# One PSUM bank for X, Y and N; four score tiles; score matmuls of two heads in turns

## The chip, the cores and the metric

The kernel runs on one core of a Trainium2 chip. A core has five engines with queues of their own: TensorE (PE in the profile; its weight loads are listed as PEld), VectorE (DVE), ScalarE (ACT), GpSimd (POOL) and SyncE (SP), which here only issues DMAs. TensorE writes its results to PSUM, an on-chip memory that this kernel fills with eight tiles, each a bank of up to 512 fp32 columns over 128 partitions. In this kernel DVE and ACT read and write PSUM; POOL and the DMAs work on the other on-chip memory, SBUF. The metric is the device time of one execution in microseconds (us).

## What is computed

Input x is 4 sequences of 512 positions with 512 channels; cond is one 512-vector per sequence. Three layers, each added to its input, stand one behind the other:

```python
# 1. attention, 16 heads of 32: q and k are RMS-normed per head
qkv  = (rms_norm(x, g_norm) * (1 + scale) + shift) @ W_qkv   # scale, shift = split(cond @ W_emb + b_emb)
o    = softmax(q @ k.T * 32**-0.5) @ v
x1   = x + o + o @ W_out
# 2. GRU over the 512 positions, one after the other; state starts at cond
gi, gh = x1[:, t] @ W_ih + b_ih, h @ W_hh + b_hh
r, z = sigmoid(i_r + h_r), sigmoid(i_z + h_z)
n    = tanh(i_n + r * h_n)
h    = (1 - z) * n + z * h
x2   = x1 + hs
# 3. two causal convolutions over time, 4 taps taken from cond, each added; the second has a bias
x3   = x2 + conv(x2, cond);  out = x3 + conv(x3, cond) + b
```

The GRU is sequential: position t + 1 needs the state of position t. Attention of a block of positions needs K and V of all positions, but Q of its own block alone.

## The kernel before

**Stages.** A first stage normalises x, builds K and V for all positions and splits the weights into fp16 pairs. Then the attention of block 0 is run (a block is 32 positions of all 4 sequences, so 128 rows; there are 16 blocks). Then come the 512 steps of the GRU (the loop at L1180, 'the scan'). Attention, output projection and input gates of blocks 1 to 15 and the convolutions of finished blocks are put between the steps.

**One step of the scan.** The program emits, in this order:
1. Fillers for DVE, ACT and POOL (`q_.head`, L1196).
2. 32 matmuls into `X` (gates r and z, L1203 to L1206), then 32 into `Y` (gate n, L1209 to L1212). They add onto a seed that ACT wrote into the same columns in the step before. Four matmuls with 32 output partitions each go side by side.
3. DVE transposes `X` into `TX` (L1214) and adds two halves into `S` (L1216). ACT takes the tanh, `ZT` (L1217), writes the next seed into `X` (`seedX`, L1219, with the instruction at L1099), and makes `d0` (L1220).
4. DVE transposes `Y` into `TY` (L1226) and combines it with ZT in a scan whose result `NN` lies in PSUM (L1227). ACT takes the tanh of NN (`D1`, L1228) and writes the next seed into `Y` (`seedY`, L1231, with the instruction at L1102).
5. TensorE's fillers (`q_.pe`, L1235) and, where they have few columns, a matmul of zeros that keeps TensorE busy (`keep_warm`, L1236, with the instruction at L241).
6. DVE makes the new state: `A` (L1237) and `HS` (L1238). The next step's matmuls into `X` need A.

**PSUM.** `X`, `NN` and `Yb` (with `Y` in its first 128 columns and `idle`, a place for matmuls of zeros, in the rest) are three tiles, and each tile takes a bank. Two banks are tiles with tag `m` (transposes, projections), two with tag `s` (scores), one with tag `O` (attention output).

**What orders the accesses.** The program has no semaphores written by hand. The framework records for each tile which engine reads or writes it, in program order, and makes the waits.

**Planner.** `Queue` (L58) holds tasks sorted by priority. A task acquires tiles by tag, has chunks for TensorE, each with a cost in the planner's own units, and then stages on DVE, ACT or POOL with a budget per step (L37). In a step, `pe` (L128) issues chunks in order of priority as long as their costs fit into `SLOT0` = 1300 units for the first 64 steps and `PE_SLOT` = 1150 after them. The tasks of a block's attention: Q and R (queries and their norms), for each of 16 heads S (scores: three chunks of four matmuls with 32 x 512 results, one per sequence; then a row maximum `mx` on DVE at L442 and an exponential on ACT at L451), TP (transposes, then a copy on ACT at L471) and AV (the product with V), at the end ON, TO, WO and GI (output projection, gates). A block that isn't done in time is flushed: its rest is issued at once (L190). The attention of block 0 runs through the same planner before the scan, with 1300 units per round (L1060).

**The end of block 0.** `tail` (L597) projects block 0 in four column groups j: `wo(j)` writes columns j of the PSUM tile `pw` (L520, L521, L631), `x1(j)` reads columns j three times: ACT at L634, DVE at L635, ACT at L636.

Of the kernel before, what the change touches and what calls it, by code (L numbers as in the profile page):

```python
# [8 lines left out]
F32 = mybir.dt.float32  # L9
# [7 lines left out]
P = 128  # L17
# [2 lines left out]
WS = 256.0  # L20
IWS = 1.0 / WS
KS_SCALE = 32.0
PE_SLOT = 1150
SC_ = 100
SLOT0, NS0 = 1300, 64
OFF2 = 120
WARM = 384
GI_T = 2
# [4 lines left out]
          TX=(245, 0), LK=(159, 1.1), S=(4, 4.8), TP=(52, 4.7), AV=(115, 2.6))  # L33
PR1 = dict(PR, ON=(305, 0), TO=(-313, 0), WO=(-28, 0), GI=(-131, 0),
           LK=(128, 0.3), S=(67, 5.1), TP=(100, 6.1), AV=(-432, 6.6))
COLS = {SC_: 192, 230: 256, 138: 192, 137: 64, 109: 128, 330: 128, 111: 256, 108: 256}
DVE_B, ACT_B, POOL_B = 1130, 1900, 3300  # L37


# [123 lines left out]
def body(ctx, tc, x, cond, W_emb, b_emb, g_norm, W_qkv, g_q, g_k, W_out, W_ih, W_hh, b_ih, b_hh, L3_b, out):  # L163
    nc = tc.nc
# [4 lines left out]
    pg = ctx.enter_context(tc.tile_pool(name="pg", bufs=1, space=PS))  # L169
    pb = ctx.enter_context(tc.tile_pool(name="pb", bufs=1, space=PS))  # L170

    X = pg.tile([P, 256], F32, name="X")
    NN = pg.tile([P, 16, 4], F32, name="N")
    Yb = pg.tile([P, 512], F32, name="Y")
    Y, idle = Yb[:, 0:128], Yb[:, 128:512]

    def pm(name):
        return pb.tile([P, 512], F32, name=name, tag="m", bufs=2)
# [59 lines left out]
    def keep_warm(n, to=None):  # L238

        for _ in range(n):  # L240
            nc.tensor.matmul(idle if to is None else to, zz[:, 0:128], zz[:, 0:384], start=to is not None, stop=True, skip_group_check=True)  # L241

    nc.tensor.matmul(Yb, zz[:, 0:128], zz, start=True, stop=True, skip_group_check=True)
    clear()

    XD = [drm.tile([P, 2, 4, B, P], F16, name=f"XD{k}") for k in range(4)]
# [65 lines left out]

    X1, XN_, XT_ = {}, {}, {}
    last = dict(S=[], TP=[], R=[])
    q_ = Queue(dict(m=2, s=2, O=1, P=4, PT=4, xb=3, xhl=1, QS=3, q=1, o=1, gi=1, x1=3, L=3))

    def block_tasks(i):
        first, pre_q = i == 0, i < 2
        tl = []
        s = {}  # L320
# [23 lines left out]
        def turn(dst, src, tag="m"):  # L344

            def piece(j):
                def f():
                    if j == 0:
                        s[dst] = pb.tile([P, 512], F32, name="pt_", tag=tag, bufs=2)
                    transpose4(s[dst], s[src], (j,))  # L350
                return f
            return [(109, piece(j)) for j in range(4)]

        MMS = [(a, w, k) for a, w in ((0, 0), (1, 0), (0, 1)) for k in range(4)]

# [22 lines left out]
            nc.vector.scalar_tensor_tensor(s["ql"], f4, IWS, s["qh"], ALU.mult, ALU.subtract)  # L378

        if not pre_q:  # L380
            Q = add(f"Q{i}", deps=[XT_[i // 4]] + last["R"], acq=["m", "q", "QS"], chunks=[(111, qch(j, u)) for j in range(4) for u in range(6)],
                    stages=[[("ACT", 960, qs0)], [("DVE", 600, qs1)]], rel=["m"] + (["xhl"] if i % 4 == 3 else []))

        def rch():
# [40 lines left out]
        prev_av = None  # L425

        def sch(j, q, u):
            def f():
                if u == 0:
                    s[("s", j, q)] = pb.tile([P, 512], F32, name="ps", tag="s", bufs=2)  # L430
                t = s[("s", j, q)]
                R_ = slice(32 * q, 32 * q + 32)
                x_, k_ = (("qh", KH), ("qh", KL), ("ql", KH))[u]
                for b in range(B):
                    nc.tensor.matmul(t[32 * b:32 * b + 32, :], s[x_][R_, j, 32 * b:32 * b + 32], k_[R_, j, b, :],  # L435
                                     start=(u == 0), stop=(u == 2), skip_group_check=True)
            return f

        def smax(j, q):
# [15 lines left out]
        def tpch(h, ps=False):  # L455
            def piece(j):
                def f():
                    if j == 0:
                        s[("pt", h)] = pb.tile([P, 512], F32, name="ptp", tag="s" if ps else "m", bufs=2)
                    transpose4(s[("pt", h)], s["PX"][h], (j,))  # L460
                return f
            return [(109, piece(j)) for j in range(4)]

        def tps(h):
            def f():
# [18 lines left out]
        for j in range(4):  # L484
            for q in range(4):
                h = 4 * j + q
                STask[h] = add(f"S{i}.{h}", h, deps=[R], acq=["s", "P"], after=last["S"], chunks=[(SC_, sch(j, q, u)) for u in range(3)],
                               stages=[[("DVE", 600, smax(j, q)), ("Pool", 150, lambda: None)], [("ACT", 720, sexp(j, q))]],
                               rel=["s"], settle=int(first))
                last["S"] = [STask[h]]  # L490
                TPs[h] = add(f"TP{i}.{h}", h, deps=[STask[h]], after=last["TP"], acq=["m", "PT"], chunks=tpch(h),
                             stages=[[("ACT", 490, tps(h))]], rel=["m", "P"], settle=int(first))
                last["TP"] = [TPs[h]]
                dep = [TPs[h]] + ([prev_av] if prev_av else [])
                AVs[h] = add(f"AV{i}.{h}", h, deps=dep, chunks=[(137, avch(h, kt)) for kt in range(4)],
                             acq=["O"] if h == 0 else [], rel=["PT"])
                prev_av = AVs[h]
# [49 lines left out]
        def chain():  # L547
            ON = add(f"ON{i}", deps=[AVs[15]], acq=["o"], stages=[[("DVE", 800, on)]], stage_lag=[1], rel=["O", "QS", "L"])

            TO = add(f"TO{i}", deps=[ON], acq=["m"], chunks=turn("pto", "o"), stages=[[("ACT", 480, tos), ("DVE", 600, lambda: None)]], rel=["m"], settle=1)  # L550
            WO = add(f"WO{i}", deps=[TO, LX], acq=["m", "x1"], chunks=[(230 if u < 0 else 111, woch(j, u)) for j in range(4) for u in range(-1, 6)],
                     stages=[[("ACT", 960, wos)], [("DVE", 600, wos1)]], rel=["m", "xb", "o"], settle=1)

            gis = []
            for g, n in enumerate("rzn"):
                def gch(g, n, part):
                    def f():
                        if part == 0:
                            s["pgi" + n] = pm("pgi")
                        c = slice(256 * (part // 12), 256 * (part // 12) + 256)  # L560
                        a, wi, k = MMS[part % 12]
                        nc.tensor.matmul(s["pgi" + n][:, c], s[("x1h", "x1l")[a]][:, k, :], WR[n][:, wi, k, c],
                                         start=(part % 12 == 0), stop=(part % 12 == 11))
                    return f

                def gst(g, n):
                    def f():
                        gs = at("gs", [P, 4, P])
                        pj = "p (j q s) -> p q j s"
                        nc.vector.tensor_tensor(gs.rearrange("p q (j s) -> p q j s", j=4), s["pgi" + n].rearrange(pj, j=4, q=4),  # L570
                                                bias[:, g].rearrange(pj, j=4, q=4), ALU.add)
                        nc.sync.dma_start(GD[i][:, :, :, g, :].rearrange("q b t c -> (b t) q c"), gs)
                    return f

                gis.append(add(f"GI{i}{n}", deps=[WO], acq=["m", "gi"], chunks=[(108, gch(g, n, p)) for p in range(24)],
                               stages=[[("DVE", 600, gst(g, n))]], rel=["m", "gi"], settle=1))

        if first:
# [18 lines left out]
        def tail(nx, ahead):  # L597
# [42 lines left out]
            def gik(k):  # L640
                for n in "rzn":
                    if k == 0:
                        pg[n] = pm("pgn") if n == "n" else pb.tile([P, 512], F32, name="pgi" + n, tag="s", bufs=2)
                    for m, (xa, wi) in enumerate(((xh, 0), (xl, 0), (xh, 1))):
                        nc.tensor.matmul(pg[n], xa[:, k, :], WR[n][:, wi, k, :], start=(k == 0 and m == 0), stop=(k == 3 and m == 2))

# [42 lines left out]
    with ExitStack() as pre_ctx:  # L689
# [81 lines left out]
            nc.scalar.activation(YS[i], XS[i], AF.Copy, scale=RS[:, i:i + 1])  # L771

        def x_t(i, tag=None):
            PY[i] = pb.tile([P, 512], F32, name="py", tag=tag, bufs=2 if tag == "s" else 1) if tag else pm("py")
            transpose4(PY[i], YS[i])

        def x_n(i, e):
# [121 lines left out]
        KV4 = {}  # L899

        def proj(v, kt, b):
            p = pb.tile([P, 512], F32, name="pkv", tag="s", bufs=2)
            XH, XL = XHL[kt]
            n = 0
            for k in range(4):
                for (xa, wi) in ((XH, 0), (XL, 0), (XH, 1)):
                    nc.tensor.matmul(p, xa[:, k, b, :], WKV[:, wi, k, v, :], start=(n == 0), stop=(n == 11))
                    n += 1
            return p
# [143 lines left out]
    x2b = [lt(f"x2b{i}", [P, 16, 35]) for i in range(2)]  # L1053
    x3b = [lt(f"x3b{i}", [P, 16, 35]) for i in range(2)]
    with tc.manual_schedule(engines={ENG.PE, ENG.DVE, ENG.Activation, ENG.Pool, ENG.SP}):
        ahead = [t for t in need[1] if t.name in ("S1.0", "S1.1", "S1.2")]
        late = [t for t in need[1] if t.name == "S1.3"]
        need[1] = [t for t in need[1] if t not in ahead + late]
        q_.add(need[0] + ahead)
        q_.flush(need[0] + ahead, 1300, lambda used: keep_warm(max(0, int((800 - used) / 160))), {8: scan_constants})  # L1060
        gs0 = bts[0]["tail"](bts[1], late)
    for i in range(1, NB):
        if i > 1:
# [51 lines left out]
    def conv_tasks(i):  # L1115
# [47 lines left out]
            nc.scalar.activation(ob, s["px4"], AF.Copy)  # L1163
            nc.sync.dma_start(out[:, 32 * i:32 * i + 32, :], ob)

        TX = Task(f"TX{i}", prio=100 * i + PR["TX"][0], deps=[C1], acq=["m"], chunks=[(109, toc(j)) for j in range(4)], stages=[[("ACT", 480, tos)]], rel=["m", "cv"])
        return [C1, TX]

    q_.free["cv"] = 1
# [101 lines left out]
```

## Time and profile before

| | |
|---|---|
| median of three executions | 1899.21 us (1896.22 to 1905.69) |
| profiled execution | 1898.34 us, of it a span of 1896.6 us from the first to the last instruction |
| busy, share of the span | PE 86%, DVE 77%, ACT 62%, PEld 61%, POOL 17% |
| A (L1237), one per step | first starts at 230.9 us, last at 1877.2 us: 3.22 us per step |
| the 32 X and 32 Y matmuls of a step (L1200) | X 273 ns each, Y 220 ns each; they overlap |
| TX, TY, N (DVE) | 447, 400, 301 ns |
| seed of X, of Y (ACT) | 396, 277 ns |
| one score matmul (L435) | 377 to 388 ns; four overlap |

How to read it: the span falls into about 231 us ahead of the first state, 511 distances from one state to the next, and some 19 us after the last. An idle time that is listed with an arrow names the instruction whose end released the engine. Times of the timeline are us from the start of the span.

### The profile page before, as it was taken

The numbers are of one execution on the slowest core, as the hardware profiler recorded it, in microseconds if no ns is written. First come the engines' busy times: TensorE is split into PE (matmuls) and PEld (weight loads), VectorE is DVE, ScalarE is ACT, GpSimd is POOL, SyncE is SP. The second block draws the span as 40 slices with busy tenths as digits, with TensorE's granted clock in tenths as the row PEclk, the third lists the DMA queues.
The fourth block names the chain that finished last, engine by engine and source line by source line (L and its number), as shares of the span: only waits on it lengthen the run. The fifth ranks groups of instructions, "written<-read, shape, count | busy, mean of one in ns | idle before, by whom it ended". The sixth has DMA issues, their size and how long they took to land. (4 is left out here: it accounts for less than half of the span.)

```text
span 1896.6 us, 113881 instructions
## 1 busy us (share of the span) xinstructions
PE 1633.8 (86%) x48944; PEld 1162.2 (61%) x48944; DVE 1453.0 (77%) x5315; ACT 1176.5 (62%) x4578; POOL 329.0 (17%) x1151
## 2 busy tenths in 40 slices
PE   5789899988899999999898989999898989987553
PEld 2444567666666666666666666666666666666442
DVE  4786477877888787878787887878787878887675
ACT  4544475766677666767575766666575757664442
POOL 1361011202111212111111111111111111111111
PEclk9999999999999999999999999999999999999998
DMA  5652011010100101010101011010101000001000
GB/s 187 221 186 112 24 51 35 22 43 19 29 24 16 34 19 54 13 39 11 38 14 31 20 35 38 21 31 11 40 13 39 12 26 19 23 24 27 16 17 9
DMA packets 68919, 78.09 MB, mean 41 GB/s; under 512 B 6560, under 2 KB 54720, under 8 KB 67776
## 3 DMA queue, kind: packets, MB, share of 16 engines
q1 hardware_dynamic: 68416, 70.82, 12.1%
q8 instruction: 384, 6.29, 1.4%
q14 instruction: 119, 0.97, 0.2%
HBM read 44.58 MB, written 26.21 MB: 37 GB/s over the span
## 5 line engine op out<-in xcount | busy, mean ns | idle before, releaser
L1200 PEld LDWEIGHTS <-BT 128*8 128x8 f16 (+1 forms) x24576 | 449.7, 89 | 69.4 <-issue 4.4
L1200 PE MATMUL X<-Wlo,A 128*4 128x256 f16 x8192 | 313.2, 273 | 187.8 <-DVE A L1237 145.4
L1217 ACT ACTIVATE ZT<-S 128x32 f32<-128x32 f32 x512 | 134.6, 263 | 503.0 <-DVE S L1216 503.0
L1214 DVE STREAM_TRANSPOSE TX<-X 128x256 f32<-128x256 f32 x512 | 228.7, 447 | 146.6 <-PE X L1200 146.3
L1242 POOL TENSOR_SCALAR hsb<-HS 128x16 f32<-128x16 f32 x512 | 115.0, 225 | 1241.5 <-DVE HS L1238 1221.4
L1200 PEld LDWEIGHTS <-A 128*4 128x4 f16 x8192 | 151.2, 83 | 282.7 <-DVE A L1237 260.1
L1200 PE MATMUL X<-Whi,BT 128*8 128x256 f16 x8192 | 315.3, 274 | 0.2 <-issue 0.2
L1200 PE MATMUL Y<-Whi,BT 128*16 128x128 f16 x8192 | 206.3, 220 | 1.5 <-issue 1.4
L1226 DVE STREAM_TRANSPOSE TY<-Y 128x128 f32<-128x128 f32 x512 | 204.8, 400 | 3.3 <-PE Y L1200 2.1
L1200 PE MATMUL Y<-Wlo,BT 128*16 128x128 f16 x8192 | 205.3, 220 | 0.8 <-issue 0.8
L1099 ACT ACTIVATE X<-G 128x256 f32<-128x256 f32 x510 | 202.1, 396 | 2.9 <-DMA G<-GD 1.4
L451 ACT ACTIVATE PX<-ps,nb,rqs 128x512 f32<-128x512 f32 x256 | 195.4, 763 | 10.8 <-DVE nb L443 5.8
L1227 DVE TENSOR_TENSOR_SCAN N<-ZT,TY 128x64 f32<-128x64 f32 x512 | 154.1, 301 | 54.8 <-ACT D L1220 1.8
L1237 DVE TENSOR_TENSOR_SCAN A<-D,D 128x32 f16<-128x32 f32 x512 | 115.3, 225 | 94.7 <-ACT D L1228 94.2
L442 DVE TENSOR_REDUCE mx<-ps 128x1 f32<-128x512 f32 x256 | 175.0, 684 | 11.4 <-PE ps L435 11.1
L297 PE MATMUL ptp<-ident,PX 128*128 128x128 f32 x1024 | 170.0, 288 | 1.3 <-DVE gs L570 0.6
L1109 ACT ACTIVATE BT<-A 128x64 f16<-128x64 f16 x512 | 131.0, 256 | 52.8 <-DVE A L1237 2.0
L297 PEld LDWEIGHTS ptp<-ident,PX 128*128 128x128 f32 x1024 | 110.4, 142 | 78.0 <-issue 61.6
L471 ACT ACTIVATE PT<-ptp 128x512 f32<-128x512 f32 x248 | 143.3, 584 | 12.8 <-PE ptp L297 12.7
L1102 ACT ACTIVATE Y<-G 128x128 f32<-128x128 f32 x510 | 141.2, 277 | 0.5 <-issue 0.3
L479 PEld LDWEIGHTS po<-V,PT 128*32 128x32 f32 x8192 | 95.3, 111 | 57.9 <-issue 53.4
L1216 DVE TENSOR_TENSOR S<-TX 128x32 f32<-128x32 f32 x512 | 114.8, 224 | 17.5
(257 smaller groups left out, 2754.9 us busy)
## 6 DMA issues: line engine op xcount, KB each, us to landing
GD<-gs SPq DMA_DIRECT2D x45, 256.0 KB
G<-GD SPq DMA_DIRECT2D x512, 16.0 KB
G<-GD SPq DMA_DIRECT2D x512, 8.0 KB
xp<-in_x_dram SPq DMA_DIRECT2D x16, 256.0 KB
xb<-in_x_dram SPq DMA_DIRECT2D x16, 256.0 KB
xhl<-XD SPq DMA_DIRECT2D x32, 128.0 KB
out_dram<-ob SPq DMA_DIRECT2D x16, 256.0 KB
wst<-in_L_cond_W_qkv_dram SPq DMA_DIRECT2D x6, 512.0 KB
```

Source lines behind the costliest of these rows:

```text
L297: nc.tensor.transpose(dst[:, 128 * j:128 * j + 128], src[:, 128 * j:128 * j + 128], ident)
L442: nc.vector.tensor_reduce(s["mx"][:, h:h + 1], s[("s", j, q)], AX.X, ALU.max)
L451: nc.scalar.activation(pe_, s[("s", j, q)], AF.Exp, bias=s["nb"][:, h:h + 1], scale=s["rqs"][:, h:h + 1], accum_out=s["ls"][:, h:h + 1])
L471: nc.scalar.activation(pt_, s[("pt", h)], AF.Copy)
L1099: nc.scalar.activation(X.rearrange("p (g c) -> p g c", g=2), G[(t // 4) % 2][:, t % 4, 0:2, :], AF.Copy)
L1102: nc.scalar.activation(Y, G[(t // 4) % 2][:, t % 4, 2, :], AF.Copy)
L1109: nc.scalar.activation(Bt[:, :, 1:8:2, :], A[:, :, 1].rearrange("p (k b) -> p k b", k=4).unsqueeze(2).to_broadcast([P, 4, 4, 4]), AF.Copy)
L1200: nc.tensor.matmul(dst[32 * qq:32 * qq + M, :], lhs, W[:, k, cols].rearrange("p g (j q s) -> p q g j s", j=4, q=4)[:, qq], start=False, st ...
L1214: nc.vector.transpose(TX.rearrange("p a r -> p (a r)"), X)
L1217: nc.scalar.activation(zt[:, :, :, 2], S.rearrange("p (g a) -> p g a", g=2), AF.Tanh, scale=0.5 * IWS)
L1226: nc.vector.transpose(TY.rearrange("p h j b k -> p j h k b"), Y.rearrange("p (j h k b) -> p j h k b", j=4, h=2, k=4))
L1227: nc.vector.tensor_tensor_scan(f(NN), f(zt[:, 0]), TY[:, 0].rearrange("p j b k -> p (j b k)"), 0.0, ALU.mult, ALU.add)
```

## The change

`X`, `Y`, `NN` and `idle` become column ranges of one tile, `XY`, of one bank. The two banks that come free go to the tag `s`, which now has four tiles. The scores of two heads are one task for TensorE: its three chunks take eight matmuls each, the two heads' matmuls in turns; each head's maximum and exponential stay tasks of their own, which depend on the pair. The pair acquires two `s` and two `P` at once. The costs of most chunks and the budgets of a step get other numbers: 1450 units for a step (1570 in the first 64), 225 for a pair's chunk of scores in place of twice 100, 150 for a transpose in place of 109, 140 for a chunk of Q in place of 111, 680 for the first chunk of each quarter of WO in place of 230, 123 for a chunk of GI in place of 108. A matmul of zeros into `idle` has 64 columns, not 384. The order of the instructions in a step is not changed, nor are the priorities.

```diff
-PE_SLOT = 1150
-SC_ = 100
-SLOT0, NS0 = 1300, 64
+PE_SLOT = 1450
+SC_ = 225
+SLOT0, NS0 = 1570, 64
...
-COLS = {SC_: 192, 230: 256, 138: 192, 137: 64, 109: 128, 330: 128, 111: 256, 108: 256}
+COLS = {SC_: 384, 680: 256, 137: 64, 150: 128, 330: 128, 140: 256, 111: 256, 123: 256}
...
-    X = pg.tile([P, 256], F32, name="X")
-    NN = pg.tile([P, 16, 4], F32, name="N")
-    Yb = pg.tile([P, 512], F32, name="Y")
-    Y, idle = Yb[:, 0:128], Yb[:, 128:512]
+    XY = pg.tile([P, 512], F32, name="XY")
+    X, Y = XY[:, 0:256], XY[:, 256:384]
+    NN = XY[:, 384:448].rearrange("p (a k) -> p a k", k=4)
+    idle = XY[:, 448:512]
...
-            nc.tensor.matmul(idle if to is None else to, zz[:, 0:128], zz[:, 0:384], start=to is not None, stop=True, skip_group_check=True)
+            o = idle if to is None else to
+            nc.tensor.matmul(o, zz[:, 0:128], zz[:, 0:o.shape[-1]], start=to is not None, stop=True, skip_group_check=True)
...
-    q_ = Queue(dict(m=2, s=2, O=1, P=4, PT=4, xb=3, xhl=1, QS=3, q=1, o=1, gi=1, x1=3, L=3))
+    q_ = Queue(dict(m=2, s=4, O=1, P=4, PT=4, xb=3, xhl=1, QS=3, q=1, o=1, gi=1, x1=3, L=3))
...
                 if u == 0:
-                    s[("s", j, q)] = pb.tile([P, 512], F32, name="ps", tag="s", bufs=2)
-                t = s[("s", j, q)]
-                R_ = slice(32 * q, 32 * q + 32)
+                    for r in (q, q + 1):
+                        s[("s", j, r)] = pb.tile([P, 512], F32, name="ps", tag="s", bufs=4)
                 x_, k_ = (("qh", KH), ("qh", KL), ("ql", KH))[u]
                 for b in range(B):
-                    nc.tensor.matmul(t[32 * b:32 * b + 32, :], s[x_][R_, j, 32 * b:32 * b + 32], k_[R_, j, b, :],
-                                     start=(u == 0), stop=(u == 2), skip_group_check=True)
+                    for r in (q, q + 1):
+                        R_ = slice(32 * r, 32 * r + 32)
+                        nc.tensor.matmul(s[("s", j, r)][32 * b:32 * b + 32, :], s[x_][R_, j, 32 * b:32 * b + 32], k_[R_, j, b, :],
+                                         start=(u == 0), stop=(u == 2), skip_group_check=True)
...
-                STask[h] = add(f"S{i}.{h}", h, deps=[R], acq=["s", "P"], after=last["S"], chunks=[(SC_, sch(j, q, u)) for u in range(3)],
+                if q % 2 == 0:
+                    SP = add(f"SP{i}.{h}", h, deps=[R], acq=["s", "s", "P", "P"], after=last["S"], chunks=[(SC_, sch(j, q, u)) for u in range(3)], settle=1)
+                    last["S"] = [SP]
+                STask[h] = add(f"S{i}.{h}", h, deps=[SP],
                                stages=[[("DVE", 600, smax(j, q)), ("Pool", 150, lambda: None)], [("ACT", 720, sexp(j, q))]],
                                rel=["s"], settle=int(first))
-                last["S"] = [STask[h]]
...
-        ahead = [t for t in need[1] if t.name in ("S1.0", "S1.1", "S1.2")]
+        ahead = [t for t in need[1] if t.name in ("SP1.0", "S1.0", "S1.1", "SP1.2", "S1.2")]
...
-        q_.flush(need[0] + ahead, 1300, lambda used: keep_warm(max(0, int((800 - used) / 160))), {8: scan_constants})
+        q_.flush(need[0] + ahead, 1700, lambda used: keep_warm(max(0, int((1050 - used) / 160))), {8: scan_constants})
```

More of the change, by code (lines that the diff above doesn't have):

```diff
@@ L240, in keep_warm @@
         for _ in range(n):
-            nc.tensor.matmul(idle if to is None else to, zz[:, 0:128], zz[:, 0:384], start=to is not None, stop=True, skip_group_check=True)
-    nc.tensor.matmul(Yb, zz[:, 0:128], zz, start=True, stop=True, skip_group_check=True)
+            o = idle if to is None else to
+            nc.tensor.matmul(o, zz[:, 0:128], zz[:, 0:o.shape[-1]], start=to is not None, stop=True, skip_group_check=True)
+    nc.tensor.matmul(XY, zz[:, 0:128], zz, start=True, stop=True, skip_group_check=True)
     clear()
@@ L351, in piece @@
                 return f
-            return [(109, piece(j)) for j in range(4)]
+            return [(150, piece(j)) for j in range(4)]
         MMS = [(a, w, k) for a, w in ((0, 0), (1, 0), (0, 1)) for k in range(4)]
@@ L380, in block_tasks @@
         if not pre_q:
-            Q = add(f"Q{i}", deps=[XT_[i // 4]] + last["R"], acq=["m", "q", "QS"], chunks=[(111, qch(j, u)) for j in range(4) for u in range(6)],
+            Q = add(f"Q{i}", deps=[XT_[i // 4]] + last["R"], acq=["m", "q", "QS"], chunks=[(140, qch(j, u)) for j in range(4) for u in range(6)],
                     stages=[[("ACT", 960, qs0)], [("DVE", 600, qs1)]], rel=["m"] + (["xhl"] if i % 4 == 3 else []))
@@ L458, in f @@
                     if j == 0:
-                        s[("pt", h)] = pb.tile([P, 512], F32, name="ptp", tag="s" if ps else "m", bufs=2)
+                        s[("pt", h)] = pb.tile([P, 512], F32, name="ptp", tag="s" if ps else "m", bufs=4 if ps else 2)
                     transpose4(s[("pt", h)], s["PX"][h], (j,))
                 return f
-            return [(109, piece(j)) for j in range(4)]
+            return [(150, piece(j)) for j in range(4)]
         def tps(h):
@@ L550, in chain @@
             TO = add(f"TO{i}", deps=[ON], acq=["m"], chunks=turn("pto", "o"), stages=[[("ACT", 480, tos), ("DVE", 600, lambda: None)]], rel=["m"], settle=1)
-            WO = add(f"WO{i}", deps=[TO, LX], acq=["m", "x1"], chunks=[(230 if u < 0 else 111, woch(j, u)) for j in range(4) for u in range(-1, 6)],
+            WO = add(f"WO{i}", deps=[TO, LX], acq=["m", "x1"], chunks=[(680 if u < 0 else 111, woch(j, u)) for j in range(4) for u in range(-1, 6)],
                      stages=[[("ACT", 960, wos)], [("DVE", 600, wos1)]], rel=["m", "xb", "o"], settle=1)
@@ L573, in gst @@
                     return f
-                gis.append(add(f"GI{i}{n}", deps=[WO], acq=["m", "gi"], chunks=[(108, gch(g, n, p)) for p in range(24)],
+                gis.append(add(f"GI{i}{n}", deps=[WO], acq=["m", "gi"], chunks=[(123, gch(g, n, p)) for p in range(24)],
                                stages=[[("DVE", 600, gst(g, n))]], rel=["m", "gi"], settle=1))
@@ L642, in gik @@
                     if k == 0:
-                        pg[n] = pm("pgn") if n == "n" else pb.tile([P, 512], F32, name="pgi" + n, tag="s", bufs=2)
+                        pg[n] = pm("pgn") if n == "n" else pb.tile([P, 512], F32, name="pgi" + n, tag="s", bufs=4)
                     for m, (xa, wi) in enumerate(((xh, 0), (xl, 0), (xh, 1))):
@@ L773, in x_t @@
         def x_t(i, tag=None):
-            PY[i] = pb.tile([P, 512], F32, name="py", tag=tag, bufs=2 if tag == "s" else 1) if tag else pm("py")
+            PY[i] = pb.tile([P, 512], F32, name="py", tag=tag, bufs=4 if tag == "s" else 1) if tag else pm("py")
             transpose4(PY[i], YS[i])
@@ L901, in proj @@
         def proj(v, kt, b):
-            p = pb.tile([P, 512], F32, name="pkv", tag="s", bufs=2)
+            p = pb.tile([P, 512], F32, name="pkv", tag="s", bufs=4)
             XH, XL = XHL[kt]
@@ L1164, in tos @@
             nc.sync.dma_start(out[:, 32 * i:32 * i + 32, :], ob)
-        TX = Task(f"TX{i}", prio=100 * i + PR["TX"][0], deps=[C1], acq=["m"], chunks=[(109, toc(j)) for j in range(4)], stages=[[("ACT", 480, tos)]], rel=["m", "cv"])
+        TX = Task(f"TX{i}", prio=100 * i + PR["TX"][0], deps=[C1], acq=["m"], chunks=[(150, toc(j)) for j in range(4)], stages=[[("ACT", 480, tos)]], rel=["m", "cv"])
         return [C1, TX]
```

## The prediction

> **What bounds the kernel now.** I read the busy shares first: TensorE 86%, DVE 77%, which settles nothing, since the 512 steps of the scan form one chain through three engines. So I asked for the groups of A, which ends each step, and for who waits for it.
>
> ```profile
> L1237 DVE TENSOR_TENSOR_SCAN A<-D,D x512: 223/224/303, 230.9 to 1877.2; 128x32 f16<-128x32 f32 x171
> ...
>   PEld L1200: 260.1, 391
> ```
>
> From 230.9 to 1877.2 us lie 511 steps: 3.22 us each. Even the weight loads of X sit idle until A in 391 of 512 steps (260.1 us): TensorE waits for the chain, not the chain for TensorE. The timeline of a step near the end, with no attention left to fill in, shows the bare chain:
>
> ```profile
> 1852.98 0.61 PE L1200 MATMUL X<-Wlo,A 128*4 128x256 f16 x16 [1.25 <-ACT Y L1102]
> ...
> 1853.41 0.61 PE L1200 MATMUL X<-Whi,BT 128*8 128x256 f16 x16
> 1853.85 0.40 PE L1200 MATMUL Y<-Wlo,BT 128*16 128x128 f16 x16
> 1854.07 0.40 PE L1200 MATMUL Y<-Whi,BT 128*16 128x128 f16 x16
> 1854.08 0.45 DVE L1214 STREAM_TRANSPOSE TX<-X 128x256 f32<-128x256 f32 x1 [0.81 <-PE X L1200]
> ...
> 1854.56 0.19 DVE L1216 TENSOR_TENSOR S<-TX 128x32 f32<-128x32 f32 x1
> 1854.67 0.40 DVE L1226 STREAM_TRANSPOSE TY<-Y 128x128 f32<-128x128 f32 x1
> 1854.78 0.26 ACT L1217 ACTIVATE ZT<-S 128x32 f32<-128x32 f32 x1 [1.46 <-DVE S L1216]
> 1854.92 0.40 ACT L1099 ACTIVATE X<-G 128x256 f32<-128x256 f32 x1
> 1855.17 0.30 DVE L1227 TENSOR_TENSOR_SCAN N<-ZT,TY 128x64 f32<-128x64 f32 x1
> ...
> 1855.50 0.19 ACT L1228 ACTIVATE D<-N 128x16 f32<-128x16 f32 x1
> ...
> 1855.72 0.22 DVE L1237 TENSOR_TENSOR_SCAN A<-D,D 128x32 f16<-128x32 f32 x1 [0.18 <-ACT D L1228]
> ...
> 1856.00 0.61 PE L1200 MATMUL X<-Wlo,A 128*4 128x256 f16 x16 [1.26 <-DVE A L1237]
> ```
>
> See two overlaps. TX starts at 1854.08, 0.06 after the last X matmul (1853.41 + 0.61 = 1854.02), while the Y matmuls run on to 1854.47. TY reads Y from 1854.67 while ACT writes the next seed into X (1854.92 to 1855.32). The bare step is 3.02 us. The mean of 3.22 has 0.20 more: over steps 32 to 479 of the timeline, TX starts 1.21 us after the first X matmul on average, not 1.10 (DVE still has fillers, 0.11 us); X starts 0.06 us later after A than in bare steps (TensorE's fillers run over); the rest, 0.03, is a few long steps at block ends.
>
> **What one bank does to the order.** X, Y and N become column ranges of one tile, so what counts is whether the framework keeps a tile's accesses apart by columns or by bank. The end of block 0 answers, where one tile `pw` is worked off in column groups:
>
> ```profile
> 213.14 0.27 ACT L634 ACTIVATE x1h<-pw 128x128 f16<-128x128 f32 x1
> 213.44 0.29 DVE L635 SCALAR_TENSOR_TENSOR x1l<-pw,x1h 128x128 f16<-128x128 f32 x1 [1.37 <-ACT x1h L634]
> 213.76 0.28 ACT L636 ACTIVATE x<-pw 128x128 f32<-128x128 f32 x1 [0.36 <-DVE x1l L635]
> ...
> 214.09 0.49 PE L520 MATMUL pw<-wsI,xb 128*128 128x128 f32 x2 [1.07 <-ACT x L636]
> ```
>
> L636 needs nothing of L635, both only read pw; yet ACT sits idle 0.36 us until DVE is done. L520 writes the next 128 columns, which L636 doesn't touch, and waits 1.07 us for it. So accesses of one tile by different engines are put in program order, whichever columns they take. I apply that to XY.
>
> **The change part by part.** Program order is X matmuls, Y matmuls, TX, S, ZT, seed of X, d0, TY, N, D, seed of Y, A.
>
> (a) TX (DVE) must wait for the last Y matmul: 1854.47 + 0.06 = 1854.53, 0.45 later. Behind it on DVE stand S, TY, N, A and the next step's fillers; ACT's ZT waits for S.
>
> (b) TY (DVE) must wait for the seed of X (ACT). With TX at 1854.53: S at + 0.48 = 1855.01, ZT at + 0.22 = 1855.23, the seed at + 0.14 = 1855.37, done at 1855.77; TY + 0.03 (ZT's distance from the end of S) = 1855.80, where (a) alone would have it at 1855.12: another 0.68. Behind TY on DVE stand N and A; ACT's D waits for N, TensorE for A. ZT, so far due with TY, is long done.
>
> (c) From TY on as before: N + 0.50, D + 0.33, A + 0.22, next X + 0.28 = 1857.13. The bare step is 4.15 us instead of 3.02. X also has to wait for the seed of Y: that starts 0.08 after D (1855.58 after 1855.50) and lasts 0.28, so 0.36 after D, against A's end 0.44 after D: hidden by A.
>
> (d) DVE's fillers (0.11): TX now starts 1.55 us after X, and by the timeline only 19 of 448 steps of before had a later TX; on average 0.01 us remains. ACT's fillers stand before ZT, which now comes 0.45 later: 0.03 us at most. TensorE's overrun (0.06) goes: the fillers took 1.39 us a step (TensorE was busy 1310.92 of 1466 us between 334 and 1800, so 2.88 of 3.22, less 1.49 for X and Y), and between Y and the next X now lie 2.66 us (4.15 less 1.49). I keep 0.04 for all of it: 4.19 us.
>
> (e) Scores. Three chunks of a head start 0.22 us apart:
>
> ```profile
> 169.31 0.40 PE L435 MATMUL ps<-KH,qh 32*32 32x512 f16 x4
> ...
> 169.53 0.40 PE L435 MATMUL ps<-KL,qh 32*32 32x512 f16 x4
> ```
>
> That is 0.65 us a head, 10.4 us a block. Two heads in turns cost between the same (one after the other) and half (side by side, as four output groups already are): 0 to 5.2 us a block. In the scan it is worth nothing either way, since TensorE idles over 1 us a step; without that idle time it would be worth up to 0.16 us a step. Ahead of the scan TensorE is busy 8.3 to 9.7 of 10 us from 180 to 220, so there block 0 can gain up to 5; four score tiles help the same 40 us. I take 3. The Trainium skill (TensorE: Matmul & The Clock Gate, Part 3) has packed tiles start some 4 ns apart, so nearly half; no row of before has two row groups at once.
>
> (f) Budgets. Summed over a middle block, the chunks cost 35,770 units before, of 32 x 1150 = 36,800; after, 42,898 of 46,400. No more flushes than before, so no price; the DMAs that a step issues (G, eight per four steps) aren't moved and get more time.
>
> (g) The clock. TensorE idles longer. Windows of 3.41 us, with TensorE's busy time first and granted clock after POOL:
>
> ```profile
> 854.31:857.72 3.41, 2.13 (x110) 1.34 (x101) 2.84 (x9) 1.97 (x9) 1.82 (x4) 1.00 0.02 5
> 857.72:861.13 3.41, 3.41 (x76) 2.08 (x68) 2.58 (x9) 1.67 (x7) 0.45 (x2) 0.50 0.02 5
> 1779.32:1782.73 3.41, 1.76 (x65) 1.25 (x65) 2.18 (x9) 1.62 (x10) 1.84 (x4) 1.00 0.02 6
> ```
>
> 2.13 us busy, with 1.28 us idle, were followed by half the clock for one window; 1.76 us in the last block were not. At half the clock X and Y took 2.66 us (857.61 to 860.27), not 1.49: 1.17 more. A new step without fillers is busy 1.83 of 4.15 us (44%), under all that kept the clock; a window with 43% at 1707.64 lost it. If half of the 32 steps of the last block and of some 34 idle ones elsewhere (7.5% of 448) are cold, that is 33 x 1.17 = 39 us. Steps with fillers are busy 65%, in the worst windows 58 to 63%; of nine windows of before with 61 to 65%, three lost the clock. Bounds: 0 and, for one step in six besides, 39 + 0.17 x 448 x 1.17 = 128 us. I take 45, near the first kind, whose rows are plainer.
> The skill's same page (Why this matters for your kernels) has the clock drop only after idle gaps above some 3 us; by it (g) were 0 and the sum 2390, but the 1.28 us above speak against it.
>
> **Sum.** Span 1896.6 = 511 x 3.222 + 250.3. New: 250.3 + 511 x 4.19 = 2391, less 3, plus 45 = 2433; with the 1.7 us that the profiled execution has outside its span, 2435. The median stands 0.9 above that execution, which changes nothing.
>
> **The rivals.**
> A (forecast): both waits, 2435; own range 2340 to 2560 (no clock loss and 4.10 a step; 128 us of it).
> B: the waits, and every second step at half the clock all through: 2390 + 511 x 0.58 = 2690. For it: the idle time per step doubles. Against it: the last block kept its clock at 52% busy.
> C: only one of the waits appears. TX alone: 3.47 + 0.09 a step, 2070; TY alone: 3.70 + 0.15, 2220. Against it: pw shows both kinds, TensorE against ACT and ACT against DVE.
> D, the other side: columns are told apart for slices of XY, no wait appears. The bare step stays 3.02, the 0.06 of TensorE's overrun goes (448 x 0.06 = 27 us) and 3 ahead of the scan: 1870, at worst 1905. It decides if TX starts 0.06 after the last X matmul, not the last Y. Against it: the 1.07 us of L520.
>
> **How the numbers follow.** A 0.73, B 0.09, C 0.08, D 0.10. The time is A's. The range, 2280 to 2660, holds nearly all of A and the milder part of B; C and D are left out. Within 0.5% (what a measurement here can't tell from no change) only the worse end of D falls: faster 0.08, same 0.02, slower 0.90.
>
> **What would show it.** In the trace after: TX's idle time released by PE Y and not X; TY idle some 0.7 us until ACT's X (L1099's line) in nearly every step; A about 4.2 us apart; X's idle time before A well above 260 us; score chunks of eight matmuls; half the clock in the last block. Wrong if TY starts 0.1 us after S as before, or if TensorE's fillers still hold up X.

## The result and the profile after

The changed kernel takes 2542.97 us (median of four; 2535.89 to 2547.17) against 1897.72 us: 1.337 times the time of before, 95% interval 1.334 to 1.341. The forecast was 2435 us in a range of 2280 to 2660: right in sign and mechanism, 108 us short in size. The profiled execution took 2547.17 us, with a span of 2545.1 us.

I read the views in the same order as before. First the group of A and who waits for it (changed kernel; L1242 is A, L1205 the matmuls of X and Y):

```profile
L1242 DVE TENSOR_TENSOR_SCAN A<-D,D x512: 223/224/227, 232.6 to 2525.7; 128x32 f16<-128x32 f32 x171
...
  PEld L1205: 866.8, 507
```

511 steps lie between 232.6 and 2525.7 us: 4.49 us each, not 3.22. The weight loads of X sat idle for 260 us in 391 steps; now for 867 us in 507. TensorE's work was never the limit, and is less so now. The list of waits names the two places that the prediction named (L1219 is TX, L1231 TY, L1104 the seed of X):

```profile
DVE TX L1219 <- PE XY L1205: 347.3, 332, 2.9
DVE TY L1231 <- ACT XY L1104: 317.2, 510, 1.0
```

In 510 of 512 steps TY waits for ACT's write of columns that TY doesn't read; before, DVE sat idle ahead of it for 3.2 us in all. A step without attention, in the timeline of the changed kernel:

```profile
2455.09 0.61 PE L1205 MATMUL XY<-Wlo,A 128*4 128x256 f16 x16 [1.75 <-DVE HS L1243]
...
2455.53 0.61 PE L1205 MATMUL XY<-Whi,BT 128*8 128x256 f16 x16
...
2455.96 0.40 PE L1205 MATMUL XY<-Wlo,BT 128*16 128x128 f16 x16
2456.19 0.40 PE L1205 MATMUL XY<-Whi,BT 128*16 128x128 f16 x16
...
2456.71 0.45 DVE L1219 STREAM_TRANSPOSE TX<-XY 128x256 f32<-128x256 f32 x1 [1.38 <-PE XY L1205]
...
2457.55 0.39 ACT L1104 ACTIVATE XY<-G 128x256 f32<-128x256 f32 x1
...
2457.98 0.40 DVE L1231 STREAM_TRANSPOSE TY<-XY 128x128 f32<-128x128 f32 x1 [0.60 <-ACT XY L1104]
2458.41 0.30 DVE L1232 TENSOR_TENSOR_SCAN XY<-ZT,TY 128x64 f32<-128x64 f32 x1
2458.62 0.17 DVE L1234 SCALAR_TENSOR_TENSOR D<-ZT,HH 128x16 f32<-128x16 f32 x1
2458.81 0.18 ACT L1233 ACTIVATE D<-XY 128x16 f32<-128x16 f32 x1 [0.72 <-DVE D L1234]
2459.03 0.28 ACT L1107 ACTIVATE XY<-G 128x128 f32<-128x128 f32 x1
2459.03 0.22 DVE L1242 TENSOR_TENSOR_SCAN A<-D,D 128x32 f16<-128x32 f32 x1 [0.24 <-ACT D L1233]
2459.17 0.20 DVE L1243 TENSOR_TENSOR_SCAN HS<-D,D 128x32 f32<-128x32 f32 x1
...
2459.36 0.61 PE L1205 MATMUL XY<-Wlo,A 128*4 128x256 f16 x16 [2.50 <-DVE HS L1243]
```

TX starts 0.12 us after the last Y matmul (2456.19 + 0.40 = 2456.59), where it used to start while they ran. TY starts 0.04 after the seed of X is done (2457.55 + 0.39 = 2457.94). The step is 4.27 us. X starts 0.05 after the seed of Y (2459.03 + 0.28 = 2459.31), not after HS, which the profile names: HS ends at 2459.37, when X has begun.

A window-by-window view shows the clock in the last block (busy time of TensorE first, the granted clock after POOL):

```profile
2429.29:2432.71 3.42, 1.87 (x49) 1.16 (x37) 1.33 (x5) 0.68 (x3) 0.00 (x0) 0.50 0.02 5
2432.71:2436.12 3.41, 2.63 (x64) 1.95 (x64) 1.27 (x7) 0.81 (x4) 0.23 (x1) 0.50 0.00 0
2436.12:2439.53 3.41, 0.91 (x25) 0.63 (x25) 2.25 (x10) 1.48 (x7) 0.23 (x1) 1.00 0.02 5
2439.53:2442.95 3.42, 2.16 (x53) 1.36 (x41) 1.09 (x4) 0.76 (x3) 0.00 (x0) 0.50 0.10 29
```

Half the clock for two windows, one at full clock with 0.91 of 3.41 us busy, then half again. In the scan, 14% of the time passes at half the clock, in 57 stretches; before it was under 1%, in three.

The sum of the prediction, term by term, in the profiled execution (bare step: median of steps 32 to 479 that saw no half clock; clock: what the steps with half clock take above a bare one; rest: what remains above bare steps):

| | predicted | measured |
|---|---|---|
| 511 bare steps | 4.15 us, 2121 | 4.27 us, 2182 |
| fillers and long steps | 20 | 27 |
| half clock | 45 | 84 |
| ahead of the first A and after the last | 247 | 252 (232.6 + 19.4) |
| span | 2433 | 2545 |

### The profile page after: what moved, and what is told of

The parts are those of the page before. It is cut to its first block, busy times and chain, and to the rows that moved or that the text cites. A ratio compares the mean times of both kernels' runs of the same rounds, so it can differ in the third digit from the quotient of the medians.

```text
span 2545.1 us, 114074 instructions
## 1 busy us (share of the span) xinstructions
PE 1667.2 (66%) x48980; PEld 1258.3 (49%) x48980; DVE 1496.5 (59%) x5315; ACT 1214.3 (48%) x4578; POOL 326.1 (13%) x1151
## 5 line engine op out<-in xcount | busy, mean ns | idle before, releaser
L1205 PE MATMUL XY<-Wlo,A 128*4 128x256 f16 x8192 | 330.4, 284 | 795.5 <-DVE HS L1243 743.0
L1205 PEld LDWEIGHTS <-A 128*4 128x4 f16 x8192 | 181.0, 84 | 883.9 <-DVE A L1242 866.8
L1205 PE MATMUL XY<-Whi,BT 128*8 128x256 f16 (+1 forms) x16384 | 570.3, 263 | 0.0
L1205 PEld LDWEIGHTS <-BT 128*8 128x8 f16 (+1 forms) x24576 | 516.6, 95 | 58.2 <-ACT HH L1115 0.5
L1219 DVE STREAM_TRANSPOSE TX<-XY 128x256 f32<-128x256 f32 x512 | 230.2, 450 | 441.1 <-PE XY L1205 347.3
L1231 DVE STREAM_TRANSPOSE TY<-XY 128x128 f32<-128x128 f32 x512 | 205.2, 401 | 317.2 <-ACT XY L1104 317.2
L1233 ACT ACTIVATE D<-XY 128x16 f32<-128x16 f32 x512 | 94.7, 185 | 366.6 <-DVE D L1234 366.6
L1205 PE MATMUL XY<-Wlo,BT 128*16 128x128 f16 x8192 | 224.5, 234 | 0.0
L454 ACT ACTIVATE PX<-ps,nb,rqs 128x512 f32<-128x512 f32 x256 | 194.9, 761 | 16.2 <-DVE nb L446 11.4
L1104 ACT ACTIVATE XY<-G 128x256 f32<-128x256 f32 x510 | 201.7, 396 | 1.4 <-DMA G<-GD 1.2
L1242 DVE TENSOR_TENSOR_SCAN A<-D,D 128x32 f16<-128x32 f32 x512 | 114.8, 224 | 123.8 <-ACT D L1233 123.8
L1232 DVE TENSOR_TENSOR_SCAN XY<-ZT,TY 128x64 f32<-128x64 f32 x512 | 153.5, 300 | 17.8
L1107 ACT ACTIVATE XY<-G 128x128 f32<-128x128 f32 x510 | 143.3, 281 | 17.2 <-ACT D L1233 0.8
L482 PE MATMUL po<-V,PT 128*32 128x32 f32 x8192 | 124.8, 202 | 0.7
```

The costliest lines, as they stand in the source:

```text
L454: nc.scalar.activation(pe_, s[("s", j, q)], AF.Exp, bias=s["nb"][:, h:h + 1], scale=s["rqs"][:, h:h + 1], accum_out=s["ls"][:, h:h + 1])
L482: nc.tensor.matmul(s["po"][32 * b:32 * b + 32, 32 * h:32 * h + 32], s["PT"][h][:, kt, 32 * b:32 * b + 32], V[:, 4 * b + kt, 32 * h:32 * h ...
L1104: nc.scalar.activation(X.rearrange("p (g c) -> p g c", g=2), G[(t // 4) % 2][:, t % 4, 0:2, :], AF.Copy)
L1107: nc.scalar.activation(Y, G[(t // 4) % 2][:, t % 4, 2, :], AF.Copy)
L1205: nc.tensor.matmul(dst[32 * qq:32 * qq + M, :], lhs, W[:, k, cols].rearrange("p g (j q s) -> p q g j s", j=4, q=4)[:, qq], start=False, st ...
L1219: nc.vector.transpose(TX.rearrange("p a r -> p (a r)"), X)
```

## Experiments

Each is compared with the kernel before on the same chip. Where a bare step is given, it is taken from that run's timeline as in the table. The question was whether the one bank makes the loss, by which of its waits, what the other parts do, and where the 112 us beyond the sum come from.

**The bank alone, and all but the bank.**

```diff
 # e1, on the kernel before
-    X = pg.tile([P, 256], F32, name="X")
-    NN = pg.tile([P, 16, 4], F32, name="N")
-    Yb = pg.tile([P, 512], F32, name="Y")
+    XY = pg.tile([P, 512], F32, name="XY")
...
 # e2, on the changed kernel: the same lines the other way round, and
-    q_ = Queue(dict(m=2, s=4, O=1, P=4, PT=4, xb=3, xhl=1, QS=3, q=1, o=1, gi=1, x1=3, L=3))
+    q_ = Queue(dict(m=2, s=2, O=1, P=4, PT=4, xb=3, xhl=1, QS=3, q=1, o=1, gi=1, x1=3, L=3))
```

> The kernel before with X, Y, N and idle in one tile of one bank; two score tiles, single heads, the old units. Theory (the order of accesses within the bank makes the loss): bare step 4.27 us as in the changed kernel, TY idle until the seed of X in nearly all steps, 511 x 4.31 + 250 and some 40 us of half clock in the last block: 2490 us, 2450 to 2560. Rival (pairs, chunk costs or budgets make a good part of it): 2300 us or less.

Measured: 2595.0 us, 1.367 times before (1.360 to 1.374). The bare step is 4.27 us, as expected and as in the changed kernel, so the bank alone makes that step, and TY waits for the seed of X as often as there:

```profile
DVE TY L1227 <- ACT XY L1100: 317.8, 510, 1.0
```

The time was missed: it is 105 us above the forecast and out of its range. Half clock takes 134 us in it, not 40 (20% of the scan's time), and the first A comes at 237.0 us. The rest of the change thus saves 52 us next to the bank, nearly all of it at the clock (134 - 84 = 50 us). Why the clock falls more often with the old units and single heads is not shown: in steps 64 to 447 that saw no half clock, TensorE is busy 2.92 us a step on average here and 2.80 in the changed kernel, so less work in a step doesn't explain it; only its spread is wider (a tenth of these steps are under 2.57 us, there under 2.64).

> The changed kernel with X, N and Y in three banks as before, so two score tiles; pairs of heads and the new units stay (head 3 of block 1 is done ahead of the end of block 0). Theory: the step is 3.0 to 3.2 us again, 1900 us, 1860 to 1930. Rival (the pairs or the budgets cost time by themselves): above 2000 us.

Measured: 1982.5 us, 1.044 times before (1.041 to 1.048): more than the theory allowed, just short of the rival. Most steps are short (median 3.08 us, by the same count 3.19 before), but one step near each block's end takes 9.3 to 9.8 us (eleven of them, steps 93 to 413), besides 16.2 and 10.2 us at steps 29 and 61. They are flushes: a pair takes both score tiles, so the next pair can't start until both heads' exponentials are done, and the attention isn't finished in time. Two score tiles don't carry pairs. That part of the change needed its banks. e8 below, which differs from this run in a third score tile and in the place of N, has no step above 4.2 us after step 61.

**Which of the columns cost.**

```diff
 # e3, on the changed kernel (three score tiles)
+    X = pg.tile([P, 256], F32, name="X")
+    Yb = pg.tile([P, 512], F32, name="Y")
+    Y = Yb[:, 0:128]
+    NN = Yb[:, 128:192].rearrange("p (a k) -> p a k", k=4)
...
 # e4, on the changed kernel (three score tiles)
     X, Y = XY[:, 0:256], XY[:, 256:384]
-    NN = XY[:, 384:448].rearrange("p (a k) -> p a k", k=4)
+    NN = pg.tile([P, 16, 4], F32, name="N")
...
```

> The changed kernel with X in a bank of its own, Y, N and idle in another, three score tiles (head 3 of block 1 done early). Theory (only accesses of one tile are put in order, and X against Y is the pair that costs): TX waits for X alone, TY for nothing of ACT, step 3.0 to 3.2 us, 1890 us, 1850 to 1930. Rival (Y against N costs as well, through TY, N, D and the seed of Y): 0.2 us a step more, 2000 us.

Measured: 1916.9 us, 1.010 times before (1.007 to 1.013), in the theory's range. Taking X out of the bank gives back 626 of 645 us. TX starts 0.05 us after X again, TY 0.11 after S, half clock is gone from the scan:

```profile
1872.58 0.61 PE L1206 MATMUL X<-Whi,BT 128*8 128x256 f16 x16
...
1873.24 0.45 DVE L1220 STREAM_TRANSPOSE TX<-X 128x256 f32<-128x256 f32 x1 [0.81 <-PE X L1206]
...
1873.73 0.19 DVE L1222 TENSOR_TENSOR S<-TX 128x32 f32<-128x32 f32 x1
1873.84 0.40 DVE L1232 STREAM_TRANSPOSE TY<-Y 128x128 f32<-128x128 f32 x1
...
1874.09 0.40 ACT L1105 ACTIVATE X<-G 128x256 f32<-128x256 f32 x1
```

What is left in the chain is D: it starts 0.39 us after N instead of 0.33. By itself that is 31 us; the time rises by 18 (1898.5 us before on this chip), so something else, not taken apart, gives a little back.

> The changed kernel with N in a bank of its own, X and Y in one, three score tiles (head 3 of block 1 done early). Theory (D's extra wait and the seed of Y, which now has to follow D, are 0.11 us of the bare step): bare step 4.15 to 4.20 us, 2490 us, 2470 to 2515. Rival (these come from elsewhere): 2535 to 2550 us.

Measured: 2471.4 us, 1.301 times before (1.296 to 1.306). The bare step is 4.16 us: the prediction's 4.15. D in the view of its line, first in the changed kernel, then here:

```profile
L1233 ACTq EVENT_SEMAPHORE  x512: 17/17/17, 232.4 to 2525.4; - x171
...
  DVE D L1234: 366.6, 512
```

```profile
  DVE N L1232: 335.4, 512
...
  DVE A L1242: 90.6, 505
```

With N in XY, D needs a second wait, which stands as an instruction of its own in ACT's queue in all 512 steps, and it starts 0.06 us later after N. (The profile names L1234 only because it ended last before D: it stands behind D in the program, and in the step shown above the extra wait is over at 2458.76, 0.05 us after N ends and before L1234 does, at 2458.79.) The seed of Y, behind D in the same bank, starts 0.22 us after D's start and not 0.08, and so ends after A: X waits for it (0.33 us after A, not 0.28). Both are gone with N apart. The two profiled spans are 78 us apart: 0.11 us a step is 56 of them, and 26 us less at half clock (58, not 84) are the rest, less some 4 us more of fillers and long steps.

**The wait of TY, and the wait of TX.**

```diff
 # e5, on the changed kernel
-            if 1 < t + 1 < T:
-                seedX(t + 1)
             nc.scalar.activation(d0[:, :, 1], zt[:, 1, :, 2], AF.Copy, scale=-0.5, bias=0.5)
...
             if 1 < t + 1 < T:
+                seedX(t + 1)
                 seedY(t + 1)
```

> The changed kernel with ACT's seed of X moved behind D, just ahead of the seed of Y; no other edit. Theory (TY waits for the seed of X only because it stands ahead of it in the program): TY starts 0.11 us after S again, 0.7 us earlier, but the two seeds then follow D (0.40 and 0.28 us with 0.03 between) and the next X waits for them: bare step 4.0 us, 2405 us, 2370 to 2440. Rival (TY's place doesn't set the step): 2540 us or more.

Measured: 2388.1 us, 1.255 times before (1.248 to 1.263), in the theory's range. The timeline, from S to the next X:

```profile
2000.05 0.19 DVE L1221 TENSOR_TENSOR S<-TX 128x32 f32<-128x32 f32 x1
2000.15 0.40 DVE L1229 STREAM_TRANSPOSE TY<-XY 128x128 f32<-128x128 f32 x1
...
2001.05 0.19 ACT L1231 ACTIVATE D<-XY 128x16 f32<-128x16 f32 x1 [0.26 <-DVE D L1232]
2001.27 0.39 ACT L1104 ACTIVATE XY<-G 128x256 f32<-128x256 f32 x1
...
2001.69 0.28 ACT L1107 ACTIVATE XY<-G 128x128 f32<-128x128 f32 x1
...
2002.02 0.61 PE L1205 MATMUL XY<-Wlo,A 128*4 128x256 f16 x16 [1.28 <-ACT XY L1107]
```

TY follows S at once, though the seed and TY use the bank and the columns that they used: only their order in the program changed. The price comes back behind D, where both seeds stand ahead of the next X. The bare step is 4.08 us, 0.20 less; half clock takes 39 us, not 84.

```diff
 # e10, on the changed kernel: TX ahead of the Y matmuls
+            nc.vector.transpose(TX.rearrange("p a r -> p (a r)"), X)
...
             for k in range(4):
                 mm(Y, Bt[:, k, 4:8].rearrange("p s b -> p (s b)"), 16, Wlo, k, slice(2, 3))
...
-            nc.vector.transpose(TX.rearrange("p a r -> p (a r)"), X)
```

> The changed kernel with TX put ahead of the Y matmuls in the program; no other edit. Theory (each access of the bank waits for the one before it on another engine): TX starts 0.06 to 0.12 us after X, the Y matmuls then wait for TX and start 0.7 us later, the seed of X waits for them, TY for the seed: bare step 4.0 us, 2405 us, 2370 to 2450. Rival (columns decide for TensorE's writes): Y doesn't move, bare step 3.8 us, 2300 us.

Measured: 2515.0 us, 1.322 times before (1.316 to 1.328), above the theory's range. The order is the theory's, the price isn't: the bare step is 4.21, not 4.0 us.

```profile
1322.02 0.61 PE L1205 MATMUL XY<-Whi,BT 128*8 128x256 f16 x16
1323.26 0.40 PE L1205 MATMUL XY<-Wlo,BT 128*16 128x128 f16 x16 [0.62 <-DVE TX L1213]
```

The Y matmuls wait 0.62 us for TX, which reads other columns: TensorE's writes are no exception. But TX comes 0.12 us after X and not 0.06, the seed of X 0.11 after the Y matmuls, and the waits of D and X that e4 removes are still there; I had left these out. Half clock takes 70 us.

**The clock.**

```diff
 # e6, on the changed kernel
-WARM = 384
+WARM = 1920
 # e7, as e6, and
-            keep_warm(-(-(WARM - q_.cols) // 384), pm("warm")[:, 0:384] if q_.free["m"] else None)
+            if q_.free["m"]:
+                keep_warm(-(-(WARM - q_.cols) // 384), pm("warm")[:, 0:384])
```

> The changed kernel with the target for matmul columns in a step at 1920 in place of 384, so that steps with little work get up to five matmuls of zeros. Theory (half clock, 14% of the scan's time, costs some 80 us): no drops in the last two blocks, all steps near 4.3 us, 2460 us, 2440 to 2490. Rival (the clock loss lies beside other waits): 2530 us or more.

Measured: 2556.9 us, 1.344 times before (1.335 to 1.354): a miss; it looks like the rival. But the last two blocks did speed up, from 4.87 and 5.11 us a step to 4.37 and 4.41. The bare step rose from 4.27 to 4.39. The waits say why (L242 is the matmul of zeros):

```profile
PE XY L242 <- ACT XY L1107: 280.1, 191, 2.2
PE XY L1205 <- ACT XY L1107: 274.3, 186, 1.9
```

Where no `m` tile was free, the zeros went to `idle`, which now lies in the shared bank: they waited for the seed of Y, and X behind them in TensorE's queue. So the same without those:

> As the run with more matmuls of zeros, but they are issued only in steps where a tile with tag m is free for them; none goes into the shared bank during the scan. Theory (that run lost at the next X, which stood behind zeros that waited for the seed of Y, 0.12 us a step, what it gained at the clock): bare step 4.27 us again, half clock under 8% of the scan's time, 2500 us, 2480 to 2520. Rival (more matmuls of zeros don't pay wherever they go): 2540 us or more.

Measured: 2497.0 us, 1.312 times before (1.307 to 1.317), as expected. The bare step is 4.27 us again, half clock takes 27 us, not 84. The last stretch of the scan, first in the changed kernel, then here:

```profile
2200.00:2525.00 325.00, 178.06 (x4342) 125.51 (x4340) 146.75 (x591) 99.91 (x461) 20.59 (x79) 0.72 0.04 11
```

```profile
2140.00:2464.00 324.00, 198.50 (x5465) 141.14 (x5454) 166.61 (x666) 119.10 (x536) 23.21 (x91) 0.96 0.04 12
```

TensorE's busy time goes up by 20 us, the clock from 0.72 to 0.96, and the kernel gets 46 us shorter: this share of the loss lay on the path.

**Can the rest of the change pay without the bank?** N in SBUF leaves X and Y a bank each and three for scores.

```diff
 # e8, on the changed kernel (three score tiles)
+    X = pg.tile([P, 256], F32, name="X")
+    NN = cst.tile([P, 16, 4], F32, name="N")
+    Yb = pg.tile([P, 512], F32, name="Y")
...
 # e9, on the kernel before (three score tiles)
-    NN = pg.tile([P, 16, 4], F32, name="N")
+    NN = cst.tile([P, 16, 4], F32, name="N")
...
```

> The changed kernel with X and Y in a bank each and N in SBUF, three score tiles (head 3 of block 1 done early). Theory (with Y and N apart, D's extra wait of 0.06 us goes from each step; reading N from SBUF costs D up to 0.04): bare step 3.02 to 3.06 us, 1885 us, 1865 to 1905, so 10 to 50 under the run with Y and N in one bank. Rival (that run is held up by its three score tiles or budgets): 1910 us or more.

> The kernel before with N in SBUF and the bank given to a third score tile; single heads, the old units. If the third tile alone lets the fillers run earlier: 1885 us, 1870 to 1897. If it makes no difference: 1895 to 1905; if N in SBUF costs D 0.04 us a step: 1915.

Measured: e8 1909.3 us, 1.004 times before (1.002 to 1.007); e9 1900.7 us, 1.000 (0.998 to 1.002). e8 lies between its theory and its rival: D starts 0.07 us earlier after N than in e3, but takes 0.04 longer when it reads SBUF, so the gain on e3 is 8 us, close to the noise (their intervals touch). e9 shows no net effect: reading N from SBUF makes its chain 0.03 us a step longer, some 17 us in all, yet the time stays; whether the third tile gives that back was not taken apart. Pairs with the new units are no better than single heads, with the same three tiles and N in the same place (3.25 against 3.23 us a step). None of the runs is faster than the kernel before.

## Why the prediction was right, and where it fell short

**The order by bank** was read off four lines at the end of block 0 and held: TX behind Y, TY behind the seed of X, in nearly every step. e1 shows the bank alone makes the bare step, e3 and e4 that X against Y is what costs, e5 and e10 that the program's order decides and columns don't. Rivals C and D are out: both waits appear, and no columns of XY are told apart. Only the wording, "accesses of one tile by different engines are put in program order, whichever columns they take", is too wide. D (L1233) and L1234 write different columns of `D1`, a tile in SBUF, and L1234, behind D in the program, starts 0.19 us ahead of it in the step shown (2458.62 against 2458.81). What the runs show is the order for tiles in PSUM. The Trainium skill (PSUM — Partial Sum Buffer, PSUM bank collisions raise a hardware error) asks for a guard by bank and partition quadrant between any two engines, whatever the columns. The waits between engines here agree with it by bank; no run tells quadrants apart, and what comes without the waits was not tried.

**Step (c), the bare step of 4.15 us,** was 0.12 short, 61 of the 112 us. With N apart (e4) it is 4.16. The failing clause was "X also has to wait for the seed of Y ...: hidden by A". I took the seed's start from before, 0.08 us after D's start, where two ACT instructions overlap because one reads N's tile and the other writes Y's. In one bank the seed waits for D, starts 0.22 after it and ends 0.06 after A, so X starts 0.33 us after A's start and not 0.28. The prediction applied the order by bank to pairs of engines and not to two instructions of one engine. The other half is D's second wait (0.06). TX's second wait (it starts 0.12 us after Y, not 0.06) is about made up by TY to N, 0.43 instead of 0.50 us, where a wait went.

**Step (g), the clock,** was taken at 45 us and measured 84, inside its bounds of 0 and 128. That longer idle time costs clock, and most of all in the last block, was right. Mis-sized was the number of steps: it counted 33 at 1.17 us, half of the last 32 and half of 34 elsewhere, and a little on top. 90 steps see half clock, at 0.94 us each on average. 27 of them lie in block 15 (26 us; 67% of its time at half clock) and 22 in block 14 (19 us; 48%), where the planner has run ahead: the last matmul of gates stands in step 459, before in step 472, and the steps behind it have no attention left. The other blocks hold 41 (39 us; 2 to 18% of a block's time).

How long TensorE is busy in a window doesn't decide it. Two windows of the changed kernel, each with the next one:

```profile
282.31:285.72 3.41, 2.15 (x98) 1.23 (x90) 1.78 (x8) 1.87 (x8) 0.11 (x1) 1.00 0.09 27
285.72:289.14 3.42, 3.42 (x70) 2.70 (x70) 1.40 (x4) 0.98 (x4) 0.41 (x2) 0.50 0.02 5
2483.91:2487.32 3.41, 1.35 (x64) 1.27 (x64) 1.31 (x7) 1.56 (x7) 0.22 (x1) 1.00 0.00 0
2487.32:2490.74 3.42, 0.92 (x33) 0.60 (x25) 1.94 (x8) 1.48 (x7) 0.22 (x1) 1.00 0.03 7
```

2.15 us busy lost the clock, 1.35 us kept it. In the scan, the 57 windows at full clock that were followed by half of it were 26 to 63% busy, and 296 with under 65% kept it; in e1 a window with 69% lost it. The prediction's "of nine windows of before with 61 to 65%, three lost the clock" is also misread: of the windows at full clock up to 1701 us it was two of eight (the next one that lost it, at 1707.64, was 43% busy), and the 19 such windows behind them all kept it. In all these traces the clock changes only on a grid of 3.41 us; what in a window decides it stays open. The Trainium skill (TensorE: Matmul & The Clock Gate, Why this matters for your kernels) ties a loss of clock to gaps above some 3 us between matmuls; here TensorE was never idle for more than 2.7 us in the scan, and the clock fell all the same.

**Steps (d), (e), (f)** held in the scan. DVE's fillers vanish behind TX's wait (27 us with all else, 20 expected). The scores of two heads do run side by side, and it buys nothing:

```profile
1506.27 0.41 PE L438 MATMUL ps<-KH,qh 32*32 32x512 f16 x8
1506.50 0.40 PE L438 MATMUL ps<-KL,qh 32*32 32x512 f16 x8
1506.72 0.40 PE L438 MATMUL ps<-KH,ql 32*32 32x512 f16 x8
...
1509.66 0.61 PE L1205 MATMUL XY<-Wlo,A 128*4 128x256 f16 x16 [1.76 <-DVE HS L1243]
```

Eight matmuls start 0.22 us after the last eight, as four did. That agrees with the Trainium skill (TensorE: Matmul & The Clock Gate, Part 3), by which matmuls in different 32x32 tiles of the array run side by side. Yet TensorE then sits idle 1.76 us until the next X in this step. The 3 us that (e) took off ahead of the scan didn't come: the first A is 1.8 us later than before. One execution of each can't settle so small a term: in e7, whose code ahead of the scan is that of the changed kernel, the first A comes at 228.5 us, 4 earlier. (f) counted only the whole budget, which was enough for this kernel; e2, against e8, shows that with two tiles it is the tiles that decide and not the units.

Rival B came in a mild form: half clock took 14% of the scan's time, not every second step.

## What to carry to other kernels

Before tiles are packed into one bank, write down for the loop's critical chain which engine touches which of them in program order: with a framework that orders a PSUM tile's accesses by bank, each neighbouring pair becomes a wait, reads against reads and two instructions of one engine included. Freed banks are worth what the work they serve is worth; here TensorE had idle time already, so faster scores bought nothing. When a change lengthens a serial step, ask next what the engine that idles longer loses in clock.

## What the runs showed that was not expected

- A second semaphore to wait for is an instruction of its own (17 ns on ACT, 21 ns on DVE by the views of D's and TX's lines), but what stands behind it started about 0.06 us later: D 0.39 instead of 0.33 us after N, TX 0.12 instead of 0.06 after the matmuls. For D, e4 shows both going together; for TX no run took the second wait away alone.
- With e7's zeros in place of idle time, the mean granted clock of the whole run is 0.972 instead of 0.926; zeros in the wrong bank (e6: 0.956) cost more than they gave.
- Reading N from SBUF instead of PSUM made ACT's D 0.04 us longer, and DVE's write of N 0.01 us shorter (e8).
